# Layer 1 of a four-layer network: a memset on another engine, and a new order of transposes, keys' sums, statistics and centring

## The chip, the cores and the metric

The kernel runs on one core of a Trainium2 chip. The core has TensorE (PE, matmuls into PSUM; its weight loads are shown as PEld), VectorE (DVE), ScalarE (ACT), GpSimd (POOL) and SyncE (SP, which issues DMAs here). Each engine has a queue of its own and works it off in order; semaphores make one wait for another. The metric is the time of one execution on the device in microseconds (us), the median of several runs.

## What is computed

The input x has 2 batches of 512 channels and 32x32 pixels. Four layers follow one another: an attention with sampled keys and an MLP (layer 0), a linear attention (layer 1), and two attentions behind a group norm (layers 2 and 3). The change lies in layer 1 and in the step that leads into layer 2. Layer 1 is, for each batch (c = 512 channels, n = 1024 pixels, 64 rows in Q and K):

```python
Q = jnp.einsum('oc,bcn->bon', wq, xf) + bq[None, :, None]
K = jnp.einsum('oc,bcn->bon', wk, xf) + bk[None, :, None]
V = jnp.einsum('oc,bcn->bon', wv, xf) + bv[None, :, None]
Q = Q / jnp.linalg.norm(Q, axis=1, keepdims=True)
K = K / jnp.linalg.norm(K, axis=1, keepdims=True)
Qt = jnp.transpose(Q, (0, 2, 1))
k_sum = K.sum(axis=-1) + EPS
tailor = 1.0 / (n + jnp.einsum('bnm,bm->bn', Qt, k_sum))
v_sum = V.sum(axis=-1)
matrix = jnp.einsum('bmn,bcn->bmc', K, V)
matrix_sum = v_sum[:, :, None] + jnp.einsum('bnm,bmc->bcn', Qt, matrix)
weight_value = matrix_sum * tailor[:, None, :]
return x + gamma[0] * weight_value.reshape(b, c, h, w)
```

Layer 2 begins with a group norm, for which the mean and variance of x over each of 8 groups of 64 channels are needed.

## The kernel before, in words

x stays in the core's memory throughout, as two batches of four tiles of 128 channels by 1024 pixels (`self.xs[b][t]`), and every layer updates it in place. All arithmetic is float32.

Layer 1 (`layer1`, from line 1038) follows the MLP of layer 0 (`mlp0`, products on line 899, last x updates on 998, 1012 and, on GpSimd, 1017 to 1021). Inside a block with `manual_schedule`, the queues of TensorE, ScalarE and VectorE take their instructions in the order in which the program writes them (lines 1237 to 1279). GpSimd and SyncE aren't in that list: a scheduler orders them by priority. So GpSimd works off sums of the weights of layer 2 (`left_sums`, lines 869 to 872, tiles `qkw` and `qkm`) before and among the small steps of layer 1.

The steps, by their names in the code:

- `queries_keys(b, half)`: 32 products of x with the weights of Q and K for four blocks of 128 pixels (line 1073; each float32 product is two instructions); VectorE adds the bias on the way out of PSUM (1076). After the second half ScalarE squares the result (1084, tile `sq`).
- `means_less(b)`: ScalarE passes over the four tiles of x with a factor of -1/1024 and keeps the sum in one column of `less` (1089); what it writes besides goes to `spare`. `less` is set to zero first (1056), by GpSimd.
- `unit_length(b)`: VectorE adds the squares (1093), ScalarE takes the root (1094), VectorE the reciprocal (1095), and scales keys into `kn` (1097) and queries in place (1098).
- `keys_sum(b)`: TensorE adds `kn` over all pixels with a matrix of ones (1117), VectorE adds epsilon (1119, tile `kbs`).
- `turned_x(b, ns)`: TensorE transposes blocks of x, four transposes for each of 8 blocks (1108); the block is copied out of PSUM by ScalarE, or for some by VectorE (1111). For batch 0 VectorE has the odd blocks. The blocks alternate between two pools of three PSUM banks, `ps` and `ps_q`.
- `divided(b)`: the division by n plus the product with the keys' sum, on GpSimd and VectorE (1124 to 1132).
- `keys_x(b)`: TensorE multiplies `kn` with the transposed x (1141), ScalarE copies the result (1149). `centred(b)`: TensorE turns it (1155), and VectorE takes the mean of x times the keys' sum off it (1158, tile `m1c`). `matrix(b)`: TensorE multiplies with the weights of V (1181), VectorE finishes `mat` (1191).
- `means_row`, `means_columns`: the sum of V from the means in `less`. `turned(b, h)`: the queries turned (1170).
- `result(b, j, h)`: two products (1221); one is added to x by VectorE (1227), the other goes by ScalarE (1231, tile `ws`) to GpSimd, which adds it to x (1232).
- `channel_means(2, 0, t)`: VectorE's statistics of one tile of x for the norm of layer 2 (1517, 1518). `group_means`: a generator in two steps: an average over each group by TensorE (1527) and four small VectorE steps (1529 to 1532); then a second average (1534), a root on ScalarE (1535) and two VectorE steps (1536, 1537). `norm_first`: three small VectorE steps (1546 to 1548) and the first normed blocks of layer 2, on VectorE (1568) and ScalarE (1560).

Layer 2 begins with products of these first blocks and the weights `qkw` (line 1385, tile `qk20P`).

Of the kernel before, what the change touches and what calls it, by code (L numbers as in the profile page):

```python
# [22 lines left out]
NB = N // P  # L23
# [33 lines left out]
class Net:  # L57
# [980 lines left out]
    def layer1(self, w, bias):  # L1038
# [3 lines left out]
        with ExitStack() as ctx:  # L1042
# [10 lines left out]
            vec, act, gps = nc.vector, nc.scalar, nc.gpsimd  # L1053
            spare = pool.tile([P, N], F32, tag="spare", name="l1spare")
            less = pool.tile([P, CT, 32], F32, tag="less", name="l1less")
            gps.memset(less, 0.0)
            pick = pool.tile([P, B], F32, tag="pick", name="l1pick")
            gps.tensor_tensor(pick, self.ident[:, 0:B], self.ident[:, 32 : 32 + B], ALU.add)
            for at in (64, 96):
# [4 lines left out]
            def queries_keys(b, half):  # L1064

                if half == 0:
                    qk.append(pool.tile([P, NB, 2, DH], F32, tag=f"qk{b}", name=f"qk{b}"))
                qk_ps = ps_q.tile([P, 4, P], F32, tag="ps", name=f"l1qk{b}{half}")
                for i in range(4):
                    n = 4 * half + i  # L1070
                    for t in range(CT):
                        xt = self.xs[b][t][:, n * P : (n + 1) * P]
                        nc.tensor.matmul(
                            qk_ps[:, i, :], lhsT=xt, rhs=w[:, t, C:640], start=(t == 0), stop=(t == CT - 1)
                        )
                vec.tensor_tensor(
                    qk[b][:, 4 * half : 4 * half + 4, :, :].rearrange("p n a d -> p n (a d)"),
                    qk_ps,
                    bias[:, C:640].unsqueeze(1).to_broadcast([P, 4, P]),
                    ALU.add,  # L1080
                )
                if half:
                    sqs.append(pool.tile([P, NB, 2, DH], F32, tag=f"sq{b}", name=f"sq{b}"))
                    act.activation(sqs[b], qk[b], AF.Square)

            def means_less(b):

                for t in range(CT):
                    act.activation(spare, self.xs[b][t], AF.Copy, scale=-1.0 / N, accum_out=less[:, t, b : b + 1])

            def unit_length(b):
                r = small.tile([P, NB, 2], F32, tag="r", name=f"r{b}")
                vec.tensor_reduce(r, sqs[b], AX.X, ALU.add)
                act.activation(r, r, AF.Sqrt)
                vec.reciprocal(r, r)
                kn.append(pool.tile([P, NB, DH], F32, tag=f"kn{b}", name=f"kn{b}"))
                vec.tensor_tensor(kn[b], qk[b][:, :, 1, :], r[:, :, 1:2].to_broadcast([P, NB, DH]), ALU.mult)
                vec.tensor_tensor(
                    qk[b][:, :, 0, :], qk[b][:, :, 0, :], r[:, :, 0:1].to_broadcast([P, NB, DH]), ALU.mult
                )  # L1100

            def turned_x(b, ns):
                if b == len(xT):
                    xT.append(pool.tile([P, NB, C], F32, tag=f"xT{b}", name=f"xT{b}"))
                for n in ns:
                    tr = (ps, ps_q)[n % 2].tile([P, C], F32, tag="ps", name=f"l1t{b}{n}")
                    for t in range(CT):
                        nc.tensor.transpose(
                            tr[:, t * P : (t + 1) * P], self.xs[b][t][:, n * P : (n + 1) * P], self.ident
                        )  # L1110
                    (vec.tensor_copy if n % (2 + 2 * b) == 1 else act.copy)(xT[b][:, n, :], tr)

            def keys_sum(b):

                kb_ps = ps_m.tile([P, DH], F32, tag="s", name=f"kb{b}")
                for n in range(NB):
                    nc.tensor.matmul(kb_ps, lhsT=ones, rhs=kn[b][:, n, :], start=(n == 0), stop=(n == NB - 1))
                kbs.append(small.tile([P, DH], F32, tag="kb", name=f"kbs{b}"))
                vec.tensor_scalar(kbs[b], kb_ps, 1e-6, None, ALU.add)

            def divided(b):

                prod = sqs[b][:, :, 0, :]
                gps.tensor_tensor(prod, qk[b][:, :, 0, :], kbs[b].unsqueeze(1).to_broadcast([P, NB, DH]), ALU.mult)
                d = small.tile([P, NB], F32, tag="d", name=f"d{b}")
                vec.tensor_reduce(d, prod, AX.X, ALU.add)
                vec.tensor_scalar(d, d, float(N), None, ALU.add)
                vec.reciprocal(d, d)
                vec.tensor_scalar(d, d, self.col("gamma1"), None, ALU.mult)
                qn.append(pool.tile([P, NB, 2, DH], F32, tag=f"qn{b}", name=f"qn{b}"))  # L1130
                for i in range(2):
                    gps.tensor_tensor(
                        qn[b][:, :, i, :], qk[b][:, :, 0, :], d.unsqueeze(2).to_broadcast([P, NB, DH]), ALU.mult
                    )
# [61 lines left out]
            def means_row():  # L1196

                got = ps_m.tile([P, C], F32, tag="s", name="l1row")
                for t in range(CT):
                    nc.tensor.matmul(  # L1200
                        got[32 * t : 32 * t + 32, :], lhsT=less[:, t, :], rhs=w[:, t, 0:C], start=True, stop=True
                    )
                row = pool.tile([P, C], F32, tag="row", name="l1rows")
                act.copy(row, got)
                return row
# [10 lines left out]
            def result(b, j, h):  # L1216
                for half, to in enumerate((ps, ps_q)):
                    t = 2 * half + j
                    rows = slice(half * DH, (half + 1) * DH)
                    w_ps = to.tile([P, HF], F32, tag="ps", name=f"w{b}{h}{t}")  # L1220
                    nc.tensor.matmul(
                        w_ps, lhsT=mats[b][rows, j * P : (j + 1) * P], rhs=q_at[2 * b + h][rows, :], start=True, stop=True
                    )
                    xt = self.xs[b][t][:, h * HF : (h + 1) * HF]
                    more = rest[:, b, t : t + 1]
                    if half == 0:
                        vec.scalar_tensor_tensor(xt, w_ps, more, xt, ALU.add, ALU.add)
                    else:

                        ws = last.tile([P, HF], F32, tag="ws", name=f"ws{b}{h}{t}")  # L1230
                        act.activation(ws, w_ps, AF.Identity, bias=more)
                        gps.tensor_tensor(xt, xt, ws, ALU.add)
# [2 lines left out]
            self.first = {2: self.first_block(2, 0)}  # L1235
            engines = {getattr(mybir.EngineType, e) for e in ("PE", "Activation", "DVE")}
            with self.tc.manual_schedule(engines=engines):
                queries_keys(0, 0)
                means_less(0)
                queries_keys(0, 1)  # L1240
                queries_keys(1, 0)
                unit_length(0)
                means_less(1)
                queries_keys(1, 1)
                keys_sum(0)
                turned_x(0, range(NB))
                unit_length(1)
                divided(0)
                keys_x(0)
                row = means_row()  # L1250
                turned_x(1, range(0, 4))
                centred(0)
                keys_sum(1)
                turned_x(1, range(4, NB))
                matrix(0)
                turned(0, 0)
                turned(0, 1)
                means_columns(row)
                divided(1)
                for j in range(2):  # L1260
                    for h in range(2):
                        result(0, j, h)
                keys_x(1)
                for t in (0, 2):
                    self.channel_means(2, 0, t)
                turned(1, 0)
                turned(1, 1)
                centred(1)
                for t in (1, 3):
                    self.channel_means(2, 0, t)  # L1270
                matrix(1)
                steps = self.group_means(2, 0, ps_m.tile([P, 2, 5 * CT], F32, tag="s", name="gm2"))
                result(1, 0, 0)
                next(steps)
                result(1, 0, 1)
                next(steps, None)
                result(1, 1, 0)
                self.norm_first(2)
                result(1, 1, 1)

# [789 lines left out]
```

## Time and profile before

| | us |
|---|---|
| median of 3 runs (3251.33 to 3252.86) | 3251.7 |
| the profiled execution | 3251.48 |
| its span, first to last instruction | 3249.7 |
| TensorE busy | 3230.7 |
| GpSimd busy | 2351.6 |
| VectorE busy | 2388.3 |
| ScalarE busy | 1960.0 |
| layer 1, first product of line 1073 to first product of line 1385 | 2342.28 to 2397.98 |

The profile page gives the busy time of each engine and the costliest groups of instructions for the whole span. Layer 1 is 55.7 us of 3249.7, so its instructions hardly show on the page. They are read from views of the trace that can be cut to a stretch: the chain of waits (the chain of work that ended last, followed back), the timeline of one engine, and the busy time and granted TensorE clock of chosen stretches. Times in these views are counted from the start of the span. The time of an execution is a little longer than its span: 3251.48 against 3249.7.

### The profile page before, as it was taken

The numbers are of one execution on the slowest core, as the hardware profiler recorded it, in microseconds if no ns is written. First come the engines' busy times: TensorE is split into PE (matmuls) and PEld (weight loads), VectorE is DVE, ScalarE is ACT, GpSimd is POOL, SyncE is SP. The second block draws the span as 40 slices with busy tenths as digits, with TensorE's granted clock in tenths as the row PEclk, the third lists the DMA queues.
The fourth block names the chain that finished last, engine by engine and source line by source line (L and its number), as shares of the span: only waits on it lengthen the run. The fifth ranks groups of instructions, "written<-read, shape, count | busy, mean of one in ns | idle before, by whom it ended". The sixth has DMA issues, their size and how long they took to land.

```text
span 3249.7 us, 59022 instructions
## 1 busy us (share of the span) xinstructions
PE 3230.7 (99%) x24436; PEld 1200.2 (37%) x24436; DVE 2388.3 (73%) x2745; ACT 1960.0 (60%) x2032; POOL 2351.6 (72%) x1563
## 2 busy tenths in 40 slices
PE   9999999999999999999999999999999999999999
PEld 4333333333333333333333334444555533455333
DVE  7877878878877677878877765575465689855897
ACT  7787887887887587887887751111131466213662
POOL 7998999999998698998999973433333458634575
PEclk9999999999999999999999999999999999999999
DMA  6676776667766566676666761111000100000001
GB/s 172 144 151 136 154 148 144 144 145 146 148 147 132 104 149 137 139 153 140 147 145 144 150 163 67 52 39 39 0 1 1 40 1 1 15 1 14 1 1 53
DMA packets 96571, 309.35 MB, mean 95 GB/s; under 512 B 14688, under 2 KB 16864, under 8 KB 93216
## 3 DMA queue, kind: packets, MB, share of 16 engines
q0 software_dynamic: 57040, 200.31, 32.6%
q1 hardware_dynamic: 38240, 103.05, 9.8%
q8 instruction: 197, 3.23, 0.4%
q10 hardware_dynamic: 1008, 2.06, 0.2%
q14 instruction: 86, 0.70, 0.1%
HBM read 67.34 MB, written 4.46 MB: 22 GB/s over the span
## 4 chain that ended last, share of the span: by engine, by line
PE 80%; POOL 11%; DVE 6%; issue 2%; ACT 1%; DMA 0%; DVEq 0%; POOLq 0%; ACTq 0%; SPq 0%
PE hp L704 41%; PE s L1610 5%; PE o L1639 5%; POOL h L723 4%; POOL h L720 4%; PE qk30P L1385 1%; PE qk20P L1385 1%; PE qk21P L1385 1%; PE m_6P L899 1%; PE m_4P L899 1%; PE m_2P L899 1%; PE m_0P L899 1%; PE qk31P L1385 1%; PE m_5P L899 1%; PE m_3P L899 1%
## 5 line engine op out<-in xcount | busy, mean ns | idle before, releaser
L704 PE MATMUL hp<-h,w2s 128*32 128x512 f32 x16384 | 1784.0, 593 | 0.5 <-DVE h L680 0.2
L680 DVE CUSTOM_DVE_ANT_1 h<-tx,bank 128x1024 f32<-128x1024 f32 (+1 forms) x1028 | 1180.4, 1211 | 299.8 <-PE hp L704 238.2
L709 ACT ACTIVATE h<-hp,magb 128x1024 f32<-128x1024 f32 x1024 | 1132.6, 1110 | 379.4 <-PE hp L704 368.7
L704 PEld LDWEIGHTS hp<-h,w2s 128*32 128x32 f32 x16384 | 531.3, 110 | 1211.9 <-issue 1184.9
L720 POOL TENSOR_TENSOR h<-h,h 128x1024 f32<-128x1024 f32 x255 | 816.6, 3203 | 1.5 <-ACT h L709 1.5
L723 POOL TENSOR_TENSOR h<-h,h 128x1024 f32<-128x1024 f32 x254 | 748.5, 2947 | 1.7 <-DMA h<-h 1.6
L716 POOL DMA_DIRECT2D h<-h x255 | 302.4, 1186 | 192.3 <-ACT h L709 179.3
L1614 ACT ACTIVATE e<-s 128x1024 f32<-128x1024 f32 x256 | 261.8, 1025 | 181.0 <-PE s L1610 175.1
L711 ACT ACTIVATE h<-h,flip 128x1024 f32<-128x1024 f32 x256 | 294.4, 1150 | 8.4
L1639 PE MATMUL o<-e,v 64*64 64x512 f32 x2048 | 265.3, 590 | 2.2 <-DVE q L1678 2.2
L1610 PE MATMUL s<-q,k 64*64 64x512 f32 x2048 | 266.0, 591 | 0.0
L1621 POOL TENSOR_TENSOR some<-some,e 128x1024 f32<-128x1024 f32 x64 | 167.6, 2619 | 26.7 <-ACT e L1614 24.2
L1619 POOL TENSOR_TENSOR some<-e,e 128x1024 f32<-128x1024 f32 x32 | 76.1, 2378 | 141.3 <-DVE sum L1628 106.3
L726 POOL DMA_DIRECT2D h<-h x127 | 175.3, 1381 | 1.0 <-issue 1.0
L725 POOL DMA_DIRECT2D h<-h x127 | 148.5, 1169 | 0.0
L1626 DVE TENSOR_TENSOR sum<-sum,e 128x1024 f32<-128x1024 f32 x64 | 123.9, 1936 | 29.9 <-ACT e L1614 26.8
L869 POOL TENSOR_TENSOR mlp_w<-mlp_w 128x512 f32<-128x512 f32 x16 | 21.2, 1325 | 164.8 <-DMA mlp_w<-in_mlp_w 140.4
L1639 PEld LDWEIGHTS o<-e,v 64*64 64x64 f32 x2048 | 77.9, 133 | 144.9 <-issue 134.8
L1610 PEld LDWEIGHTS s<-q,k 64*64 64x64 f32 x2048 | 76.6, 133 | 133.1 <-issue 117.2
L960 ACT ACTIVATE mh<-mh,cols 128x512 f32<-128x512 f32 x64 | 46.1, 721 | 124.3 <-DVE mh L978 65.4
L1373 POOL TENSOR_TENSOR sq<-q 128x512 f32<-128x512 f32 x32 | 33.2, 1039 | 99.2 <-DVE q L1392 55.1
L1624 DVE TENSOR_TENSOR sum<-e,e 128x1024 f32<-128x1024 f32 x32 | 80.8, 2524 | 32.0 <-ACT e L1614 32.0
(582 smaller groups left out, 3358.6 us busy)
## 6 DMA issues: line engine op xcount, KB each, us to landing
h<-h POOLq DMA_DIRECT2D x255, 512.0 KB, 5.4
h<-h POOLq DMA_DIRECT2D x254, 256.0 KB, 5.0
h<-h SPq DMA_DIRECT2D x127, 256.0 KB, 4.0
lb<-logs SPq DMA_DIRECT2D x63, 512.0 KB, 5.8
mlp_w<-in_mlp_w SPq DMA_DIRECT2D x16, 1024.0 KB, 5.0
x<-in_x SPq DMA_DIRECT2D x8, 512.0 KB, 7.5
qkw<-in_l_qk SPq DMA_DIRECT2D x2, 2048.0 KB, 8.0
out<-x SPq DMA_DIRECT2D x15, 256.0 KB, 2.1
```

The source lines that it names most:

```text
L680: self.nc.vector._custom_dve(TENSOR_ADD_SAT, out=h1[r][:, k, cut, :], in0=x[:, 4 * half + 2 * r + k, :].unsqueeze(1).to_broadcast([P, H // ...
L704: nc.tensor.matmul(hp[rows, cut], lhsT=self.l0w2[:, 32 * q : 32 * q + 32], rhs=h1[k][:, cut], start=True, stop=True)
L709: nc.scalar.activation(y, hp, AF.Relu, bias=self.magb[:, q, 0:1])
L711: nc.scalar.activation(y, y, AF.Copy, scale=self.flip)
L716: nc.gpsimd.dma_start(y, ys[0], accum_op=ALU.add)
L720: (nc.vector if final else nc.gpsimd).tensor_tensor(y, y, ys[2], ALU.add)
L723: (nc.vector if final else nc.gpsimd).tensor_tensor(z, z, other, ALU.add)
L726: nc.gpsimd.dma_start(z[1::2, :], z[0::2, :], accum_op=ALU.add)
L899: self.nc.tensor.matmul(acc[p], lhsT=w[:, a, k, p * P : (p + 1) * P], rhs=right(r, k), start=k == 0, stop=k == 1)
L1610: nc.tensor.matmul(s[halves[c], par, :], lhsT=ks[p][rows, at : at + DH], rhs=qs[p][rows, cut], start=True, stop=True)
L1614: nc.scalar.activation(e, s, AF.Exp, scale=DH**-0.5)
L1639: nc.tensor.matmul(o[halves[par], r, :], lhsT=v[n // 2][rows, n % 2, at : at + DH], rhs=e[rows, par, :], start=(n == 0), stop=(n == NB - 1),)
```

## The change

One memset moves from GpSimd to VectorE, and calls in the order of layer 1 are moved: `means_less(0)` ahead of `queries_keys(0, 0)`; half of the first batch's transposes ahead of `keys_sum(0)`; the statistics of tile 1 ahead of `turned` and `centred` of the second batch; the first step of `group_means` ahead of `result(1, 0, 0)`; its second step ahead of `result(1, 0, 1)`; and `norm_first` ahead of both results of tile 1. No computation is added or left out.

```diff
@@ -1053,7 +1053,7 @@
             vec, act, gps = nc.vector, nc.scalar, nc.gpsimd
             spare = pool.tile([P, N], F32, tag="spare", name="l1spare")
             less = pool.tile([P, CT, 32], F32, tag="less", name="l1less")
-            gps.memset(less, 0.0)
+            vec.memset(less, 0.0)
             pick = pool.tile([P, B], F32, tag="pick", name="l1pick")
@@ -1235,15 +1235,16 @@
             with self.tc.manual_schedule(engines=engines):
+                means_less(0)
                 queries_keys(0, 0)
-                means_less(0)
                 queries_keys(0, 1)
                 queries_keys(1, 0)
                 unit_length(0)
                 means_less(1)
                 queries_keys(1, 1)
+                turned_x(0, range(0, 4))
                 keys_sum(0)
-                turned_x(0, range(NB))
+                turned_x(0, range(4, NB))
                 unit_length(1)
                 divided(0)
                 keys_x(0)
@@ -1261,22 +1262,21 @@
                 keys_x(1)
-                for t in (0, 2):
+                for t in (0, 2, 1):
                     self.channel_means(2, 0, t)
                 turned(1, 0)
                 turned(1, 1)
                 centred(1)
-                for t in (1, 3):
-                    self.channel_means(2, 0, t)
+                self.channel_means(2, 0, 3)
                 matrix(1)
                 steps = self.group_means(2, 0, ps_m.tile([P, 2, 5 * CT], F32, tag="s", name="gm2"))
+                next(steps)
                 result(1, 0, 0)
-                next(steps)
+                next(steps, None)
                 result(1, 0, 1)
-                next(steps, None)
-                result(1, 1, 0)
                 self.norm_first(2)
-                result(1, 1, 1)
+                for h in range(2):
+                    result(1, 1, h)
```

## The prediction, made before the result was known

> **What bounds the kernel now.** I read the page first: TensorE is busy for 99% of the span, so an edit counts only where TensorE waits, or where its clock is low. The change touches layer 1 alone, so I went to the chain of waits in that stretch, in order of time (start, length, what).
>
> ```profile
> 2342.14 2.37 POOL qkm L869
> 2344.57 2.36 POOL qkw L870
> 2347.01 2.35 POOL qkm L871
> 2349.67 1.16 ACT l1spare L1089 x2
> ...
> 2354.37 0.95 ACT sq L1084
> 2355.33 1.28 ACT L1094
> ...
> 2358.00 1.97 PE kb L1117 x16
> 2359.97 5.17 PE l1t L1108 x32
> ...
> 2387.57 0.86 DVE m1c L1158 x4
> 2388.43 1.21 DVE stats L1517 x2
> 2389.87 1.16 DVE stats L1517 x2
> 2391.26 0.28 DVE mat L1191
> ```
>
> The chain leaves TensorE twice. At the front it runs through GpSimd's sums for the next layer (qkm, qkw), then the sums of x on ScalarE (l1spare), the squares, a table load, and returns with the keys' sum at 2358.00. At the end it runs through VectorE's centring and statistics. How long TensorE really stands still is in its own timeline, with ScalarE's beside it (start, length, line, shape; in brackets the idle time before it and what ended it).
>
> ```profile
> 2349.67 1.06 ACT L1089 ACTIVATE l1spare<-x 128x1024 f32<-128x1024 f32 x1 [27.15 <-POOL l1less L1056]
> 2358.00 1.97 PE L1117 MATMUL kb<-kn,l1ones 128*128 128x64 f32 x16 [1.26 <-DVE kn L1097]
> 2359.80 5.33 PE L1108 MATMUL l1t<-ident,x 128*128 128x128 f32 x32
> 2369.66 1.97 PE L1108 MATMUL l1t<-ident,x 128*128 128x128 f32 x16
> 2397.98 4.53 PE L1385 MATMUL qk20P<-xn,qkw 128*128 128x512 f32 x10 [1.20 <-DVE xn L1568]
> ```
>
> ScalarE is idle for 27 us and starts only when GpSimd's memset of `less`, queued behind three sums of 2.35 us, is done. TensorE loses 1.26 us on kn. From 2358.00 to 2388.2 it has no gap, then gaps of 1.04, 1.16 and 1.20 us. And 32 transposes take 5.26 us from start to next start, where 16 later take 1.81. The windows say why (stretch, length, busy us of PE, PEld, DVE, ACT, POOL with counts, granted clock, DMA).
>
> ```profile
> 2356.50:2359.90 3.40, 2.14 (x20) 1.98 (x19) 2.21 (x5) 3.33 (x7) 0.00 (x0) 1.00 0.00 0
> 2359.90:2363.30 3.40, 3.40 (x18) 3.40 (x17) 0.92 (x2) 3.37 (x7) 1.27 (x1) 0.51 0.00 0
> 2363.30:2366.70 3.40, 3.40 (x32) 2.72 (x33) 2.91 (x4) 1.20 (x3) 0.00 (x0) 0.99 0.02 5
> 2390.50:2393.90 3.40, 2.24 (x9) 1.19 (x10) 2.48 (x8) 0.63 (x1) 0.00 (x0) 1.00 0.00 0
> ```
>
> One stretch of 3.4 us ran at half clock, just after the stretch with the 1.26 us gap. The reader is to see 18 instructions there and 32 in the next stretch.
>
> [...] the window before the dip was only about a third idle; the tail window, with 2.24 us busy, drew no dip. [...] the clock came back at 2363.3 after a window that held transposes alone. [...]
>
> **The change part by part.** Times are those of the old trace unless called new.
>
> (1) The memset of `less` goes from GpSimd (0.20 us) to VectorE. VectorE's nearest row is a 128x64 memset of 0.11 us, so I take 0.2. It stands behind the MLP's last x update, 2342.55 + 0.69 = 2343.24, and before qk's first eviction at 2346.05: VectorE has a hole of 2.8 us there, which hides it. If its memory is released later it would hold up that eviction; TensorE has two more banks, so this begins to cost only some 7 us later. ScalarE's other release falls at the MLP's end, near 2342.4, so it starts at 2343.5, not 2349.67. Moving means_less(0) ahead of queries_keys(0, 0) moves nothing in itself: that step has no ScalarE instruction. Four sums at 1.185 us end at 2348.2. The squares now wait for qk's second eviction, 2349.63 + 0.69 = 2350.32, and end at 2351.4 (old 2355.3); the table load ends at 2352.7. What is late next is VectorE: the reduction of squares stands behind qk's third eviction, started at 2353.20 and followed 0.6 later. Reduction 2353.8 to 2355.0 (1.22), root at 2355.1 (old 2356.63), kn ready at 2356.3 (old 2357.85). So the gain on ScalarE is 1.55 us, not 6, and any memset up to about 2347 gives the same.
>
> (2) TensorE would be free for its next start at 2356.55 (128 starts of 0.1114 us from 2342.28). It goes straight into transposes of blocks 0 to 3, which need only x; the gap goes, worth 2358.00 - 2356.55 = 1.45 us. Keys' sum follows at its old 1.8 us, with kn long there.
>
> (3) Without the gap I expect no half clock. The nearest case is the second batch, where the same keys' sum stands between transposes (2369.66 to 2375.26) at full clock. 32 transposes then take 2 x 1.81 = 3.62, not 5.26: 1.64 us more. Not all of it is kept: blocks 0 to 3 end at 2358.4, keys' sum at 2360.1, blocks 4 and 5 at 2361.0; block 6 needs the buffer of block 0, which ScalarE copies only after the second batch's sums and squares. These end 1.55 earlier than before, so the copy ends at 2362.28 - 1.55 + 0.55 = 2361.3. TensorE waits 0.3, ends block 7 at 2362.25, and keys_x(0) starts there: 2365.06 - 2362.25 = 2.8 us gained. VectorE's reduction for the second batch follows block 7's copy and moves with it; until 2388 TensorE has no gap, so the 2.8 is carried on.
>
> (4) The tail, in old times. channel_means(1), 1.4 us, now stands ahead of centring: it ends at 2387.75 where centring began at 2387.57, so centring, and matrix(1) behind it on TensorE, are 0.18 late. Only one statistic (1.4) is left between centring and mat. mat was held by the second until 2391.18 though matrix(1) had ended at 2390.52; now it waits for 2390.70 and starts at 2390.75: 0.43 won. Group means then go before result(1, 0, 0): their four VectorE steps (0.6) end near 2392.15, inside the wait for the first w, whose x update comes at 2392.36. The second average follows that w at 2392.6 and ends at 2393.0; ScalarE takes the root behind its first ws, at 2393.43, where it stood at 2395.26. From the root on the order is the same (reciprocal, scale, one x update, offsets, xn: 2.72 us to TensorE's start at 2397.98). So 1.83 us. TensorE's own w products, 12 pieces of 0.233 after 2392.95, end before 2396.1, so they don't set the start. The last two ws now come after xn, and GpSimd's last x update ends at 2399.1 instead of 2399.73; blocks of xn that wait for it are wanted only 6.9 us after the start. Nothing else waits.
>
> Sum: 2.8 + 1.8 = 4.6 us. From 2398 on the old chain is TensorE without a wait, and what VectorE bounds at the very end starts from it, so the gain reaches the end. The profiled execution took 3251.48 us (span 3249.7 and 1.8 around it), 0.2 below the median of 3251.7. 3251.5 - 4.6 = 3246.9; against the median 3247.1.
>
> Bounds of the unknowns: the clock, 0 to 1.64 us lost; block 6's wait, 0 to 0.7 if ScalarE is later; memset, 0 to 1.45 if it doesn't help kn; the tail, from 1.2 (first bank of the next layer still held by a last x update) to 2.2 (TensorE's own end at 2395.8).
>
> **Rivals.** (A) The half clock comes anyway[...]. For: it fell around such sums. Against: the gap is gone, and the second batch. Block 6's wait is then hidden: gain 1.4 + 1.8 = 3.2, 3248.5. (B) The front gives nothing, because the memset is placed late (after 2348) or ScalarE is held by another release, and block 4 on wait for its copies; or the tail gives nothing because a bank or GpSimd takes the wait's place. One part remains: 1.8 to 2.8, about 3249.4. Against: the hole at 2343.24, and evictions ahead of the start in my tail. (C) Slower: [...] Both batches then run at half clock, three windows more than now at 1.64 each, 4.9 us, while the dip there stays: 3251.7 - 3.2 + 4.9 = 3253.4. It decides once more than two extra windows fall. Against: the return at 2363.3.
>
> **How the numbers follow.** Forecast 0.62, A 0.18, B 0.14, C 0.06. The range: below, the whole 5.3 us of gaps and clock plus 0.7 of spread between runs, 3245.4, set at 3245.2; above, through A and most of B, 3250.2. C and B's end stay out. A change under 0.2% (6.5 us) can hardly be told from none here: faster than 3245.2 needs more than the gaps I found, 0.07; slower than 3258.2 needs C with more windows, 0.02; between, 0.91.
>
> **What would show it.** ScalarE's first l1spare near 2343.5; no idle before the first l1t, and no half clock in layer 1; keys_x(0) near 2362.3; one statistic between m1c and mat; the root near 2390.6 and qk20P's first product near 2393.4 (old times less 4.6). A first l1spare still near 2349, a clock of 0.5 over the transposes, or qk20P waiting for an x update would make it wrong.

## The result, and the profile after

The changed kernel takes 3247.03 us (median of 22 runs, 3246.34 to 3247.81) where the kernel before takes 3251.34 beside it (22 runs). The ratio is 0.9987, with a 95% interval of 0.9981 to 0.9993: a gain of 4.3 us (4.6 was forecast), clear of no change, and below 0.2%. The profiled execution took 3246.86 us with a span of 3245.0.

TensorE's timeline of the changed kernel (start, length, line, shape; in brackets the idle time before and what ended it):

```profile
2342.51 14.45 PE L1073 MATMUL l1qk<-l1w,x 128*128 128x128 f32 x128
2356.80 1.91 PE L1108 MATMUL l1t<-ident,x 128*128 128x128 f32 x16
2358.54 1.90 PE L1117 MATMUL kb<-kn,l1ones 128*128 128x64 f32 x16
2360.28 1.04 PE L1108 MATMUL l1t<-ident,x 128*128 128x128 f32 x8
2361.61 1.09 PE L1108 MATMUL l1t<-ident,x 128*128 128x128 f32 x8 [0.29 <-ACT xT L1111]
2362.63 3.67 PE L1141 MATMUL m<-xT,kn 128*64 128x256 f32 x32
...
2386.24 1.95 PE L1181 MATMUL m<-l1w,m1c 128*64 128x256 f32 x16 [1.13 <-DVE m1c L1158]
...
2388.79 1.49 PE L1221 MATMUL w<-qa,mat 64*128 64x512 f32 x4 [0.28 <-DVE mat L1191]
...
2393.71 12.68 PE L1385 MATMUL qk20P<-xn,qkw 128*128 128x512 f32 x29 [0.34 <-DVE xn L1568]
```

The 128 instructions of line 1073 are four calls of `queries_keys` with 16 products each, two instructions to a product (not 32 products, as the description of the kernel has it). TensorE's two waits in the middle of the tail, in the profile of before:

```profile
2388.57 1.95 PE L1181 MATMUL m<-l1w,m1c 128*64 128x256 f32 x16 [1.04 <-DVE m1c L1158]
2391.68 1.48 PE L1221 MATMUL w<-qa,mat 64*128 64x512 f32 x4 [1.16 <-DVE mat L1191]
```

Four places answer to the lines of before. The wait for kn is gone, and in its place stands a short one for ScalarE's copy of a transposed block. The wait for m1c stayed (1.04, now 1.13), that for mat fell from 1.16 to 0.28, that for xn from 1.20 to 0.34. The stretch that held the front's gap (2.14 us of TensorE work in 3.40) now has no idle time, and runs at full clock (stretch, length, busy us of PE, PEld, DVE, ACT, POOL with counts, granted clock, DMA):

```profile
2356.50:2359.90 3.40, 3.40 (x34) 3.40 (x33) 2.59 (x5) 3.25 (x6) 0.00 (x0) 1.00 0.00 0
```

ScalarE's and VectorE's timelines of the same execution show what leads there:

```profile
2343.69 1.06 ACT L1089 ACTIVATE l1spare<-x 128x1024 f32<-128x1024 f32 x1 [20.94 <-DVE l1less L1056]
2360.04 1.04 ACT L1084 ACTIVATE sq<-qk 128x1024 f32<-128x1024 f32 x1
2360.99 2.02 ACT L1111 COPY xT<-l1t 128x512 f32<-128x512 f32 x4
```

```profile
2343.44 0.17 DVE L1056 MEMSET l1less<- 128x128 f32 x1
...
2385.30 0.80 DVE L1158 SCALAR_TENSOR_TENSOR m1c<-kbs,l1less,m1t 128x64 f32<-128x64 f32 x4
2386.02 1.28 DVE L1517 BATCH_NORM_STATS2 stats<-x 128x6 f32<-128x512 f32 x2
2387.33 0.21 DVE L1518 BATCH_NORM_AGGREGATE mv<-stats 128x2 f32<-128x12 f32 x1
2388.23 0.87 DVE L1191 SCALAR_TENSOR_TENSOR mat<-l1b,m 64x256 f32<-64x256 f32 x2 [0.69 <-PE m L1181]
```

The memset runs in the hole behind the MLP and ScalarE starts 0.08 us later. One statistic stands between m1c and mat, and VectorE now waits 0.69 us for matrix(1).

From here on two counts are used, both free of when layer 1 begins: from the first product of line 1073 to the first of keys_x (the front), and to the first of line 1385 (the whole). Before they are 22.78 and 55.70 us, after 20.12 and 51.20. So layer 1 is 4.50 shorter: 2.66 in the front, 1.84 behind it. The rest of the 4.7 in the spans is not the change: layer 1 began 0.23 later, and the stores after the last x update took 4.85 instead of 5.33, a time that lay between 4.76 and 5.33 in all profiled executions of this study.

### The profile page after: what moved, and what is told of

The parts are those of the page before. It is cut to its first block, busy times and chain, and to the rows that moved or that the text cites. A ratio compares the mean times of both kernels' runs of the same rounds, so it can differ in the third digit from the quotient of the medians.

```text
span 3245.0 us, 59023 instructions
## 1 busy us (share of the span) xinstructions
PE 3229.1 (100%) x24436; PEld 1197.7 (37%) x24436; DVE 2387.8 (74%) x2746; ACT 1959.6 (60%) x2032; POOL 2352.1 (72%) x1562
## 4 chain that ended last, share of the span: by engine, by line
PE 80%; POOL 11%; DVE 6%; issue 2%; ACT 1%; DMA 0%; DVEq 0%; POOLq 0%; ACTq 0%; SPq 0%
PE hp L704 41%; PE s L1610 5%; PE o L1639 5%; POOL h L723 4%; POOL h L720 4%; PE qk20P L1385 1%; PE qk30P L1385 1%; PE qk31P L1385 1%; PE m_7P L899 1%; PE m_6P L899 1%; PE m_4P L899 1%; PE m_2P L899 1%; PE m_0P L899 1%; PE qk21P L1385 1%; PE m_5P L899 1%
```

## The experiments

### The two parts, and the two edits of the front

Each of these is the kernel before with some hunks of the change: `front_alone` has the memset and all moves before `keys_x(0)`; `tail_alone` has those behind `keys_x(1)`. The other two divide the front:

```diff
 memset_alone
-            gps.memset(less, 0.0)
+            vec.memset(less, 0.0)
...
+                means_less(0)
                 queries_keys(0, 0)
-                means_less(0)

 transposes_alone
+                turned_x(0, range(0, 4))
                 keys_sum(0)
-                turned_x(0, range(NB))
+                turned_x(0, range(4, NB))
```

> Only the front of the change: memset on VectorE, means_less(0) first, transposes of blocks 0 to 3 ahead of the keys' sum; the tail as before. Theory (the two parts add up): from the first product of line 1073 the first product of keys_x (line 1141) comes after 20.1 us as in the changed kernel (22.78 before), no half clock in layer 1, and the first product of line 1385 after 52.9 (55.70 before, 51.20 changed); time 2.7 us under before. Rival (the tail depends on the front): the first product of line 1385 well off 52.9, by 0.5 or more.

> Only the tail of the change: statistics, group means and norm_first in the new order; the front as before. Theory: keys_x after 22.8 us with the half clock in the front still there, the first product of line 1385 after 53.9, time 1.8 us under before. Rival: the front's half clock is a matter of chance and not of the gap; then it may be missing here, and keys_x comes after some 21.4.

> Only the memset on VectorE and means_less(0) first; the keys' sum stays ahead of all transposes. Theory from the changed trace: kn is ready 14.0 to 14.2 us after the first product, TensorE is free at 14.29, so the gap goes without the new order of transposes, the half clock goes with it, block 6 still waits for ScalarE's copy of block 0, and keys_x comes after 20.0 to 20.2: the whole gain of the front. Rival: the transposes ahead of the sum carry part of it; then the sum waits, a gap of 0.3 or more is left, and keys_x comes after 20.5 or later.

> Only the transposes of blocks 0 to 3 ahead of the keys' sum; memset on GpSimd as before. Theory: kn comes 15.6 us after the first product, blocks 0 to 3 last until 16.0, so the gap is filled and the half clock goes; but ScalarE's sums stay late, its copy of block 0 ends only near 20.6, block 6 waits 1.5 us or more for it, and keys_x comes after 21.6 (1.2 gained). Rival (ScalarE's delay does not matter once the gap is filled): keys_x after 20.1. Second rival (the wait at block 6 brings a half clock of its own): keys_x after 22.5 or later.

Front, whole and the place of the half clock are those of the one profiled execution; the last column counts, of all executions, those with a mean clock under 1.000.

| | front, us | whole, us | half clock in layer 1 | median, us (13 runs) | mean clock under 1.000 |
|---|---|---|---|---|---|
| before | 22.78 | 55.70 | in the front | 3250.62 (41 runs) | 8 of 41 |
| front_alone | 20.13 | 53.04 | none | 3249.16 | 4 of 13 |
| tail_alone | 21.66 | 52.73 | none | 3248.84 | 5 of 13 |
| memset_alone | 20.12 | 54.63 | in the tail | 3249.54 | 5 of 13 |
| transposes_alone | 21.65 | 56.25 | behind the front | 3251.82 | 8 of 13 |

The ratios to before, with their intervals, are 0.9996 (0.9987 to 1.0004), 0.9994 (0.9985 to 1.0002), 0.9997 (0.9989 to 1.0005) and 1.0003 (0.9994 to 1.0011): none can be told from no change by time alone. The traces tell them apart.

First, the parts add up: `front_alone` gains 2.66 and meets its 20.1 and 52.9, and the tail of `tail_alone` is 1.85 shorter. In time `front_alone` was only 1.46 under before, where I expected 2.7: the 2.7 had counted a half clock that 8 of the 41 executions of before show. Second, `tail_alone` was a miss for the theory and a hit for its rival. Its front is the old one, gap included, and yet no half clock fell (TensorE's timeline with ScalarE's copy of block 0, then two stretches with their clock):

```profile
2343.03 14.46 PE L1073 MATMUL l1qk<-l1w,x 128*128 128x128 f32 x128
2358.77 1.97 PE L1117 MATMUL kb<-kn,l1ones 128*128 128x64 f32 x16 [1.29 <-DVE kn L1097]
2360.58 2.79 PE L1108 MATMUL l1t<-ident,x 128*128 128x128 f32 x24
2363.05 2.02 ACT L1111 COPY xT<-l1t 128x512 f32<-128x512 f32 x4
2363.67 1.09 PE L1108 MATMUL l1t<-ident,x 128*128 128x128 f32 x8 [0.30 <-ACT xT L1111]
2364.69 3.67 PE L1141 MATMUL m<-xT,kn 128*64 128x256 f32 x32
```

```profile
2356.50:2359.90 3.40, 2.11 (x19) 1.95 (x19) 2.99 (x5) 3.33 (x7) 0.00 (x0) 1.00 0.00 0
2359.90:2363.30 3.40, 3.40 (x32) 3.23 (x31) 1.61 (x3) 3.37 (x6) 1.28 (x1) 1.00 0.00 0
```

The reader sees the same gap and the same busy time of 2.1 us in 3.4 as in the profile of before, and a clock of 1.00 after it. This is what the front of before looks like without the half clock: 21.66 us. So in the profile of before the half clock cost 22.78 - 21.66 = 1.12 us, not 1.64, because without it block 6 waits 0.30 for ScalarE: 32 transposes take 2364.69 - 2360.58 = 4.11 us here, and not twice 1.81.

Third, `memset_alone` has the whole gain of the front: 20.12. Its keys' sum starts without a wait, with no transposes ahead of it:

```profile
2342.80 14.45 PE L1073 MATMUL l1qk<-l1w,x 128*128 128x128 f32 x128
2357.09 1.90 PE L1117 MATMUL kb<-kn,l1ones 128*128 128x64 f32 x16
2358.82 2.79 PE L1108 MATMUL l1t<-ident,x 128*128 128x128 f32 x24
2361.90 1.09 PE L1108 MATMUL l1t<-ident,x 128*128 128x128 f32 x8 [0.29 <-ACT xT L1111]
2362.92 3.67 PE L1141 MATMUL m<-xT,kn 128*64 128x256 f32 x32
```

Its two edits, the memset and the place of means_less(0), were not tried apart. ScalarE has the same instructions in the same order in its trace and in that of before, so the place of means_less(0) changed nothing in that queue. Fourth, `transposes_alone` has none of it: 21.65, against 21.66. The gap is filled, and comes back as a longer wait at block 6:

```profile
2357.32 1.91 PE L1108 MATMUL l1t<-ident,x 128*128 128x128 f32 x16
2359.07 1.90 PE L1117 MATMUL kb<-kn,l1ones 128*128 128x64 f32 x16
2360.80 1.04 PE L1108 MATMUL l1t<-ident,x 128*128 128x128 f32 x8
2363.66 1.09 PE L1108 MATMUL l1t<-ident,x 128*128 128x128 f32 x8 [1.82 <-ACT xT L1111]
2364.68 5.36 PE L1141 MATMUL m<-xT,kn 128*64 128x256 f32 x32
```

Blocks 6 and 7 start 20.63 us after the first product here and 20.64 in `tail_alone`, whatever TensorE did before. They start when ScalarE has copied block 0, behind the second batch's sums and squares: in `transposes_alone` the first block's transposes start at 2357.32 and ScalarE's copies at 2363.05, after the squares of 2362.10. The 5.36 us of keys_x (3.67 elsewhere) is a half clock after that wait, as the second rival had it; it began only after keys_x had started (clock 1.00 from 2364 to 2365, 0.52 in the next us), so it isn't in the 21.65.

### What sets the front: ScalarE's copies

If the copies bind, moving ScalarE's sums out of their way must help, with or without the memset; and a late memset must hurt. Three kernels, and the changed kernel beside them:

```diff
 sums_both_first, from the changed kernel
                 means_less(0)
+                means_less(1)
...
                 unit_length(0)
-                means_less(1)

 sums_deferred, from transposes_alone (memset on GpSimd)
                 unit_length(0)
-                means_less(1)
...
                 unit_length(1)
+                means_less(1)

 memset_late, from the changed kernel
-            vec.memset(less, 0.0)
...
-                means_less(0)
                 queries_keys(0, 0)
                 queries_keys(0, 1)
+                vec.memset(less, 0.0)
+                means_less(0)
```

> The changed kernel again, beside the next two on one chip. Theory: first product of keys_x 20.1 us and first product of line 1385 51.2 us after the first of line 1073, full clock throughout layer 1, some 3.5 to 4.3 us under before. [...]

> The changed kernel with means_less(1) directly behind means_less(0), so that ScalarE has both sums done before its first squares, and copies block 0 early. Theory (ScalarE's copies are what binds the front): kn is about 0.6 later but still ahead of its use, the wait at block 6 (0.29) goes, keys_x after 19.5, first product of line 1385 after 50.6, time 0.6 or less under the changed kernel. Rival (kn binds): kn becomes late, TensorE waits ahead of the keys' sum, and keys_x comes after 20.1 or later.

> The kernel before, memset on GpSimd and tail as before, with the transposes of blocks 0 to 3 ahead of the keys' sum, and means_less(1) moved behind unit_length(1), so that ScalarE copies block 0 before the second batch's sums. Theory: kn comes 15.6 us after the first product as before, but no copy is late: keys_x after 19.5, although the memset is as late as before; clock full in the front. Rival (the late memset itself costs): keys_x after 20.5 or later. A price may show later, in means_row, which needs the deferred sums: 0 to 0.6.

> The changed kernel with VectorE's memset and means_less(0) placed behind queries_keys(0, 1), so that the memset runs 8.0 us after the first product instead of 0.9. Theory: ScalarE's sums end near 13.0, squares 14.0, kn 16.5; TensorE waits 0.5 ahead of the keys' sum; sums of batch 1 end near 20.2 and block 6 waits for the copy until 21.8; keys_x after 22.7 (20.1 changed). Rival (slack on ScalarE covers it): keys_x within 0.3 of 20.1.

| | front, us | whole, us | median, us (runs) | ratio to before (interval) |
|---|---|---|---|---|
| changed_again | 20.12 | 51.18 | 3246.81 (21) | 0.9986 (0.9979 to 0.9993) |
| sums_both_first | 19.62 | 50.69 | 3246.63 (21) | 0.9985 (0.9978 to 0.9992) |
| sums_deferred | 19.62 | 57.38 | 3252.13 (13) | 1.0002 (0.9994 to 1.001) |
| memset_late | 22.52 | 55.08 | 3251.42 (1) | - |

Before took 3250.94 us beside them (49 runs). `memset_late` ran once, so only its trace counts. With both sums first the transposes run without a wait, and kn, though later, is not late: the keys' sum starts without one too, at 2359.13. `sums_deferred` reaches the same 19.62 with the memset as late as ever, and the old gap for kn covered by the transposes. So the late memset did not bind TensorE by itself: it bound through what stands behind the sums in ScalarE's queue. That kernel still loses, and more than I had allowed (0 to 0.6 us):

```profile
2361.57 3.67 PE L1141 MATMUL m<-xT,kn 128*64 128x256 f32 x32
2365.17 4.25 PE L1200 MATMUL l1row<-l1w,l1less 128*32 128x512 f32 x8
2369.35 1.97 PE L1108 MATMUL l1t<-ident,x 128*128 128x128 f32 x16
```

```profile
2363.53 0.21 ACT L1094 ACTIVATE r<-r 128x16 f32<-128x16 f32 x1 [1.70 <-DVE r L1093]
2363.65 1.04 ACT L1089 ACTIVATE l1spare<-x 128x1024 f32<-128x1024 f32 x1
```

The deferred sums stand behind the second root, which waits 1.70 us for VectorE; they start at 2363.65, and means_row, which needs the last of them, takes 4.25 us instead of 1.06. A half clock in the tail (0.54 from 2393.80 to 2397.20) is in its 57.38 too.

`memset_late` lost 2.40 in the front, near the 2.6 expected. One detail was wrong: the squares, written before the moved sums, went ahead of them on ScalarE, so kn was 0.2 late and not 0.5. The copy of block 0 came late all the same, and block 6 waited 2.11. A half clock followed that wait (0.83 and 0.67 in the two stretches of 3.4 us from 2363.20 on; keys_x took 5.17 us), and is in its 55.08.

### The tail, and a version with less of both waits

```diff
 statistics_alone, from the kernel before
-                for t in (0, 2):
+                for t in (0, 2, 1):
                     self.channel_means(2, 0, t)
...
-                for t in (1, 3):
-                    self.channel_means(2, 0, t)
+                self.channel_means(2, 0, 3)

 groups_alone, from the kernel before
                 steps = self.group_means(2, 0, ps_m.tile([P, 2, 5 * CT], F32, tag="s", name="gm2"))
+                next(steps)
                 result(1, 0, 0)
-                next(steps)
+                next(steps, None)
                 result(1, 0, 1)
-                next(steps, None)
-                result(1, 1, 0)
                 self.norm_first(2)
-                result(1, 1, 1)
+                for h in range(2):
+                    result(1, 1, h)

 sums_first_split, from sums_both_first
-                for t in (0, 2, 1):
+                for t in (0, 2):
                     self.channel_means(2, 0, t)
+                part = self.half_means(2, 0, 1)
+                next(part)
                 turned(1, 0)
-                turned(1, 1)
                 centred(1)
+                next(part, None)
+                turned(1, 1)
```

Here `half_means` does what `channel_means` does for a tile other than the first, but yields between its two halves.

> The kernel before with one edit: the statistics of tile 1 ahead of the second batch's centring, tile 3 alone behind it. Counted from the second batch's first keys_x product (line 1141) to the first product of line 1385: 15.36 before, 13.52 changed. Theory: mat starts about 0.43 earlier and the rest follows: 14.9. Rival (matrix(1), started 0.2 later, or the group means' place eats it): 15.2 or more. A half clock in this stretch would add some 1.6.

> The kernel before with one edit: group_means and norm_first a step earlier, the statistics in the old order. Same count as in the run beside it (15.36 before, 13.52 changed). Theory: mat stays at its old time, the root comes 1.4 earlier: 14.0. Rival (the two edits of the tail do not add up, because the means then wait for the late statistics): 14.5 or more. A half clock in this stretch would add some 1.6.

> The changed kernel with both sums first, as in the run of that name, and in the tail the statistics of tile 1 cut in two: its first half ahead of centring, which moves in front of turned(1, 1), its second half behind it. Theory (VectorE's queue binds the tail up to mat): m1c starts some 0.6 earlier, matrix(1) too, mat 0.6 earlier with no idle left before it, and the first product of line 1385 comes 50.1 us after the first of line 1073 (51.2 changed, 50.7 both sums first); time about 1.1 under the changed kernel. Rival (ScalarE's copy of m1s binds m1t): m1c not earlier than now, 50.6 or more.

> The changed kernel, on the same chip as the split version: 20.1 and 51.2 us as before, full clock, and about 1.1 us over the split version in its median.

| | from the second keys_x to line 1385, us |
|---|---|
| before | 15.36 |
| statistics_alone | 14.89 |
| groups_alone | 13.98 |
| the changed kernel | 13.52 |

0.47 and 1.38 make 1.85, and the two together gave 1.84: the edits of the tail add up. Each of the two kernels with one edit ran once; both executions have a mean clock of 1.000, and the old front of 21.6 to 21.7 us.

`sums_first_split` measured 19.61 and 50.26 us (50.1 expected), and 3245.84 us as median of 21 runs, against 3246.87 for the changed kernel beside it (21 runs): 1.03 us less, where 1.1 was expected. Its ratio to before is 0.9984 (0.9978 to 0.9991); that of the changed kernel on the same chip 0.9987 (0.9980 to 0.9994). The intervals of the two ratios overlap; the difference rests on the traces, which agree with it. TensorE's tail in it:

```profile
2384.95 1.95 PE L1181 MATMUL m<-l1w,m1c 128*64 128x256 f32 x16 [0.60 <-DVE m1c L1158]
2387.10 0.39 PE L1538 MATMUL gm<-mv,avg 128*128 128x4 f32 x2 [0.20 <-DVE mv L1521]
2387.50 1.49 PE L1221 MATMUL w<-qa,mat 64*128 64x512 f32 x4
...
2392.42 10.97 PE L1388 MATMUL qk20P<-xn,qkw 128*128 128x512 f32 x25 [0.34 <-DVE xn L1579]
```

The wait for m1c fell from 1.13 to 0.60, that for mat is gone, and a wait of 0.20 for the last statistic has taken its place: VectorE has no idle time left from m1c, at 2383.95, to the end of mat, at 2387.80.

## Why the prediction was right, point by point

The time was forecast at 3247.1 us and measured at 3247.03. This closeness is better than the working behind it, and in part luck: the gain was 4.3 where 4.6 was forecast, and before itself came out 0.4 lower in 22 runs than the 3251.7 I had started from.

**Step 1, the memset: right.** ScalarE was said to start at 2343.5 and kn to be ready at 2356.3; they came at 2343.69 and 2356.50, with layer 1 beginning 0.23 later. That a memset up to about 2347 would do as well was not tried; 8.0 us after the first product is too late, as `memset_late` shows.

**Steps 2 and 3, the front: the sum held (2.8, measured 2.66), its parts did not.** I gave 1.45 to the transposes that fill the gap and up to 1.64 to the clock, and took 0.3 off for block 6. The runs show a different cause: ScalarE's copy of block 0 ends the front's last wait, with the old front at full clock (`tail_alone`, 0.30) as with the new one (0.29), and it starts 1.54 earlier because of the memset: 20.02 us after the first product in `tail_alone`, 18.48 in the changed kernel. `memset_alone` gains 21.66 - 20.12 = 1.54, `transposes_alone` 0.01. The clock gave 1.12, and only against a profile in which it had been low. 1.54 + 1.12 = 2.66. My own step had the figure (ScalarE's sums "1.55 earlier than before") but used it for a small correction, where it was the bound. The step that failed is "the gap goes, worth 2358.00 - 2356.55 = 1.45 us": I had not asked whether block 6 waits in the kernel before as well. The half clock had hidden that wait in its trace.

**The half clock: half right.** I said that it goes with the gap. It does not always follow the gap: in three sets of runs the mean clock of before was under 1.000 in 8 of 41, 23 of 49 and 16 of 41 executions (medians 3251.76 and 3250.71 in the last set, with and without). The changed kernel showed it in none of 64. (By estimate, 3.4 us at the 0.51 of the profile of before lower the mean over 3250 us by 0.0005, so a mean rounded to thousandths just shows it.) Nor does it need the front's gap: `front_alone` and `memset_alone`, which do not have that gap, were under 1.000 in 4 and 5 of 13 executions, and the profile of `memset_alone` has the half clock in the old tail. `sums_both_first`, with the new tail and no wait in the front, was under in 1 of 21; no trace shows where. So of the 4.5 us in the traces 3.38 does not depend on the clock (1.54 + 1.84), and 1.12 is gained where a half clock would have fallen in the front. From 3250.71 to 3246.87 it is 3.84; the 0.46 above 3.38 is placed by no trace here.

**Step 4, the tail: right in size and in parts.** 1.83 was forecast, 1.84 measured; 0.43 for the statistics (0.47 alone), the rest for the earlier root (1.38 alone). No bank and no x update took the place of the waits. The prediction's "TensorE without a wait" from there on was wrong, but cost nothing: TensorE has the same waits there in both traces, 4.3 and 4.4 us in all (half of it for VectorE's q, line 1678), and from the first product of line 1385 to the last x update it took 846.39 us before, 846.44 after. Two smaller slips of the prediction: the tail's first gap begins at 2387.53 and not at 2388.2, and the four gaps and the clock make 6.3 us and not 5.3 (1.26 + 1.04 + 1.16 + 1.20 + 1.64), so its lower end was reckoned from too little.

**The rivals.** A, that the half clock comes anyway around the keys' sums, fell in 64 executions. B, that the front or the tail gives nothing, fell: alone they gave 2.66 and 1.85. The mechanism that B named is real all the same: with ScalarE held, `transposes_alone` waits 1.82 us for a copy, and the transposes give nothing by themselves. C, slower by a half clock over transposes and small sums, fell: the changed kernel's stretch from 2356.50, shown above, holds little else, and has a clock of 1.00. A kernel slower by a half clock exists all the same, but by another way: `transposes_alone`, after its wait of 1.82 us, had a mean clock under 1.000 in 8 of 13 executions (median 3252.43, the other five 3250.56) and the highest median of its set.

## What to carry to other kernels

When a wait goes, look in the trace for the next wait on the same engine before and after the edit, and ask what ends it: here ScalarE's queue, late by 1.54 us, was late for the copies behind it as well, and filling the gap for kn alone (`transposes_alone`) moved the loss to block 6, where the wait grew from 0.30 to 1.82. Before a stretch at low clock is counted as a gain, see in several executions whether it is always there (here 8 of 41 executions of before showed one). And when edits come in a bundle, their sum can be right while one of them does nothing; only runs of each alone show it.

## What the hardware showed that I had not expected

The half clock is not decided by the program alone: with one and the same program, before, 8 of 41 executions had a mean clock under 1.000 and 33 had not. Nor does the work just ahead of it settle it alone: the same front, with 2.14 and 2.11 us of TensorE busy in a stretch of 3.4, was followed by a clock of 0.51 in the profile of before and of 1.00 in that of `tail_alone`. It fell after the gap at the front (before), after the wait at block 6 (`transposes_alone`, `memset_late`), and in the tail (`sums_deferred`, `memset_alone`). In `memset_alone`:

```profile
2392.60:2396.00 3.40, 3.40 (x12) 1.55 (x10) 1.70 (x4) 1.34 (x3) 1.82 (x2) 0.62 0.00 0
```

Here 8 pieces of w took 2.91 us, where 1.99 is usual, and the tail was 1.59 longer. The half clock cost 1.12 us in before, 1.59 here and 1.69 in `transposes_alone` (5.36 - 3.67). In the five profiles that have one, the 3.4 us ahead of it held about 2.14 us of TensorE work (before), 1.59 (`transposes_alone`), 1.30 (`memset_late`) and 2.25 (`memset_alone` and `sums_deferred`); none of these stretches was idle. And before has a stretch of 3.4 us with only 1.95 in its tail, from 2388.00, and the changed kernel one with 2.26, from 2385.20. Both ran at 1.00, and so did what followed. What sets the half clock off in one execution and not in another, these runs do not show.
